# A transformer block on one core: transfers, the condition's path and weight slices of the first stage rearranged

## The chip, the cores and the metric

The kernel runs on one core of a Trainium2 chip. The metric is the device time of one execution in microseconds (us); lower is better. The engines of the core work side by side, each through its own queue in order: TensorE (PE; its weight loads are shown as PEld), VectorE (DVE), ScalarE (ACT), GpSimd (POOL) and SyncE (SP), which issues most DMAs. ScalarE and POOL issue DMAs too.

## The reference

A transformer block with a condition (adaptive layer norm), 2 batches of 2048 tokens, width D = 512, 16 heads of 32, hidden width 2048, all in f32:

```python
mod = silu(condition) @ Wada + bada
sh_a, sc_a, gt_a, sh_m, sc_m, gt_m = split(mod, 6, axis=1)
xm = layernorm(x, g1, be1) * (1.0 + sc_a[:, None, :]) + sh_a[:, None, :]
x = x + gt_a[:, None, :] * attention(xm, Wqkv, Wproj, bproj)     # causal
xm = layernorm(x, g2, be2) * (1.0 + sc_m[:, None, :]) + sh_m[:, None, :]
h = gelu(xm @ W1 + b1)
x = x + gt_m[:, None, :] * (h @ W2 + b2)
```

`condition` has 2 rows of 512, `Wada` is 512 x 3072, `Wqkv` 512 x 1536.

## The kernel before

The work is cut into tiles of 128 partitions (P). For each of the two batches there is a stage that computes queries, keys and values, then attention, then a projection; at the end comes the hidden layer for both batches. Products with weights are done by a scheme of seven products for eight (names A11, A12, A21, A22 for the four blocks of a weight, S1 to S4 for sums of blocks), so each weight block needs four sums, which POOL makes (`weight_sum`, L941) from the four loaded blocks. The change touches only the first stage, the queries, keys and values of batch 0 (L1359 to L1521).

Order: the program is written as a stream of operations; a framework places each on its engine's queue, inserts the waits, and may move an operation ahead of others on its engine, unless it is wrapped in `act` (L208), `mm` (L204) or `transpose` (L212), which keep the written order on that engine. Tiles of one tag share a fixed number of buffers, and a new one waits for the old one's last reader.

What the first stage does, in the order written:

- L89 to L152: constants, made by POOL and VectorE: the identity `ident`, masks, zeros. L136 is an activation with Sqrt on one column, `first`, that makes ScalarE load the table that holds Sqrt.
- L1363 to L1373: seven small DMAs from ScalarE's queue bring the condition (8 rows of 128), g1, be1, g2, be2, b1 and b2 as 44 rows of the tile `rows`.
- L1395 `load_x(0)`: four tiles of 128 x 512 of x, from SP. L1396 `load_wada(0, 1)`: two of the six column blocks of Wada as eight DMAs of 256 KB from SP into `vv`, and their bias from POOL into `mr`. L1397 `load_w` (L923): the four blocks of the query and key weights, 512 KB each, from SP into `wqk`. L1398 `load_wv` (L931): the value weights, four DMAs of 256 KB.
- L1400 to L1402: the 44 rows are transposed on TensorE into `ps_c` and copied to `cols`, where each vector stands as columns, by VectorE.
- L1450: for each of the four tiles of x the statistics (`stats` L216, VectorE); then `inv_std` (L223): Sqrt on ScalarE into `rstd`, its reciprocal and a product on VectorE. `scaled` (L958) normalizes the tiles on ScalarE in place, and `norm` (L970) transposes them into `ps_xt` on TensorE, in two halves of two tiles.
- L1454: Silu of the condition's columns into `sc` (ScalarE). `modulation(0)` (L1406): 16 matmuls of `sc` with Wada into `ps_mod`; `columns` (L1424): the bias added (`mr`, VectorE), eight small matmuls that turn rows into columns (`ps_modt`), a copy to `mod`. `scale_shift` (L1440) makes the factors a1 and c1 from `mod` and the columns of g1 and be1.
- L1464: `modulate` writes x, scaled, shifted and transposed, from `ps_xt` to `xmT`, even chunks on VectorE and odd ones on ScalarE. L1467: three sums of token halves (`t`, VectorE). L1469: the weight sums of columns 1 to 3 on POOL, four each; those of column 0 come later (L1477).
- L1520 `run` (L1138): for four groups of 512 tokens (g) and four weight columns of 128 (f) the products. The first column of the first group is done without the scheme (`plain`, L1086: 16 matmuls of 512 into `ps_qk`), the others with it (`unit`, L1002: seven products into banks named ps_a, ps_b, ps_c). Within `unit` the product S2 adds onto the bank of A11, after ScalarE has copied that bank out (L1059). Beside the products, `tick` (L1145) places the next group's loads of x, statistics, scaling and transposes, `also` (L1474) the later parts of the modulation, and `Pieces` (L1205) loads, sums and stores pieces of the hidden layer's weights.

Of the kernel before, what the change touches and what calls it, by code (L numbers as in the profile page):

```python
# [8 lines left out]
F32 = mybir.dt.float32  # L9
F32R = mybir.dt.float32r  # L10
BF16 = mybir.dt.bfloat16
AF = mybir.ActivationFunctionType
# [5 lines left out]
P = 128  # L18
# [9 lines left out]
def dit_block_kernel(  # L28
# [36 lines left out]
    nc = tc.nc  # L65
    B, T, D = x.shape
    HID = W1.shape[1]
    C = D // P
# [15 lines left out]
    def pool(name, bufs=1, **kw):  # L84
        return tc.tile_pool(name=name, bufs=bufs, reuse_waits="tile", **kw)
# [6 lines left out]
    ident = const.tile([P, P], F32, tag="ident", name="ident")  # L92
# [7 lines left out]
    eps = const.tile([P, 1], F32, tag="eps", name="eps")  # L100
# [16 lines left out]
    for n in range(2):  # L117

        f = bp.tile([P, QB + P], BF16, tag=f"fold{n}", name=f"fold{n}")
# [10 lines left out]
    def picks():  # L130
        two = ident.rearrange("p (k r b) -> p k r b", k=2, r=2)[:, :, :, :B]
        nc.vector.tensor_tensor(pickc, two[:, 0], two[:, 1], ALU.add)


    first = const.tile([P, 1], F32, tag="first", name="first")
    nc.scalar.activation(first, eps, AF.Sqrt)  # L136


    cols = const.tile([P, 64], F32, tag="cols", name="cols")
# [15 lines left out]
    n_cond = B * C  # L155
# [4 lines left out]
    n_rows = r_b2 + C  # L160
# [36 lines left out]
    def col(r, n):  # L197
        return cols[:, r : r + n]
# [9 lines left out]
    def act(ins):  # L208

        return tc.keep_in_program_order(ins)  # L210

    def transpose(dst, src):  # L212
        n = src.shape[0]
        return tc.keep_in_program_order(nc.tensor.transpose(dst, src, ident[:n, :n]))  # L214
# [78 lines left out]
    ps_sp = ps_s_cm.__enter__()  # L293
# [590 lines left out]
    w_v = Wqkv.rearrange("(c p) f -> p c f", p=P)  # L884
# [11 lines left out]
    HK = C // 2  # L896

    class Qkv:
# [21 lines left out]
                xts.append(xt)  # L920
            self.xts[g] = xts

        def load_w(self, queue):  # L923
            for n, i, k in BASE:
                act(
                    queue.dma_start(
                        self.w[:, n], w_v[:, k * HK : (k + 1) * HK, i * D : (i + 1) * D]
                    )
                )

# [429 lines left out]
    with pool("wada") as wp, pool("qkv0") as qp, pool("hl0") as hp, pool(  # L1360
        "ps_qkv0", bufs=6, space=PSUM
    ) as ps_mm:
        rows = wp.tile([n_rows, P], F32, tag="rows", name="rows")  # L1363
        for r, n, src in (
            (0, n_cond, cond.rearrange("b (c p) -> (b c) p", p=P)),
            (r_g1, C, g1.rearrange("(c p) -> c p", p=P)),
            (r_be1, C, be1.rearrange("(c p) -> c p", p=P)),
            (r_g2, C, g2.rearrange("(c p) -> c p", p=P)),
            (r_be2, C, be2.rearrange("(c p) -> c p", p=P)),
            (r_b1, FC, b1.rearrange("(c p) -> c p", p=P)),  # L1370
            (r_b2, C, b2.rearrange("(c p) -> c p", p=P)),
        ):
            nc.scalar.dma_start(rows[r : r + n, :], src)  # L1373
        wada_v = Wada.rearrange("(c p) f -> p c f", p=P)
        wada = {}

        def load_wada(s0, s1):
            w = row.vv[:, NT - 2 * C :].rearrange("p (n c) d -> p n c d", n=2)
            if s0 % 3 == 2:
                mr = modr  # L1380
            else:
                mr = wp.tile([P, D], F32, tag="mr", name="mr")
                nc.gpsimd.memset(mr, 0.0)
            for n, s in enumerate((s0, s1)):
                nc.gpsimd.dma_start(
                    mr[n * HD : n * HD + B, :],
                    bada[s * D : (s + 1) * D].partition_broadcast(B),
                )
            for k in range(C):
                for n, s in enumerate((s0, s1)):  # L1390
                    nc.sync.dma_start(w[:, n, k, :], wada_v[:, k, s * D : (s + 1) * D])
            wada[s0] = w, mr

        qkv = Qkv(row, qp, ps_mm)
        qkv.load_x(0)  # L1395
        load_wada(0, 1)  # L1396
        qkv.load_w(nc.sync)  # L1397
        qkv.load_wv(hp, nc.sync)  # L1398

        ps_c = ps_mm.tile([P, n_rows], F32, tag="mm", name="ps_c")  # L1400
        transpose(ps_c, rows)
        nc.vector.tensor_copy(cols[:, :n_rows], ps_c)  # L1402
        sc = wp.tile([P, C, HD], F32, tag="sc", name="sc")
        nc.vector.memset(sc, 0.0)

        def modulation(s0):  # L1406

            w, mr = wada.pop(s0)
            ps = ps_sp.tile([P, D], F32, tag="s", name="ps_mod")
            for k in range(C // 2):
                for half in range(2):
                    for n in range(2):
                        at = (2 * half + n) * HD
                        kk = half * C // 2 + k
                        mm(
                            ps[at : at + HD, :], sc[:, kk, :], w[:, n, kk, :],  # L1420
                            start=(k == 0), stop=(k == C // 2 - 1),
                        )

            def columns():  # L1424
                nc.vector.tensor_tensor(mr, ps, mr, ALU.add)
                if s0 % 3 == 2:
                    return
                ps_t = ps_sp.tile([P, C, 2, B], F32, tag="s", name="ps_modt")
                for k in range(C):
                    mm(  # L1430
                        ps_t[:, k], mr[:, k * P : (k + 1) * P], pickc,
                        start=True, stop=True,
                    )
                nc.vector.tensor_copy(
                    mod[:, s0 : s0 + 2], ps_t.rearrange("p c s b -> p s c b")
                )

            return columns

        def scale_shift(a, c, r_g, r_be, shift, scale):  # L1440

            for dst, r in ((a, r_g), (c, r_be)):
                nc.vector.scalar_tensor_tensor(
                    dst, mod[:, scale], 1.0,
                    col(r, C).unsqueeze(2).to_broadcast([P, C, B]),
                    ALU.add, ALU.mult,
                )
            nc.vector.tensor_tensor(c, c, mod[:, shift], ALU.add)

        for t in range(MTT):  # L1450
            qkv.stats(0, t)
        halves = [qkv.norm(0, 0, True)]

        act(  # L1454
            nc.scalar.activation(
                sc[:, :, :B], col(0, n_cond).rearrange("p (b c) -> p c b", c=C), AF.Silu
            )
        )
        picks()
        columns = modulation(0)  # L1460
        halves.append(qkv.norm(0, 1, True))
        columns()
        scale_shift(a1, c1, r_g1, r_be1, 0, 1)
        for k in range(0, C, 2):  # L1464
# [62 lines left out]
    with pool("qkv1") as qp, pool("ps_qkv1", bufs=6, space=PSUM) as ps_mm:  # L1527
        qkv = Qkv(row, qp, ps_mm)
# [62 lines left out]
    with ExitStack() as mlp:  # L1591
        wp = mlp.enter_context(pool("mlpw", side="right"))
        ps_mm = mlp.enter_context(pool("ps2", bufs=4, space=PSUM))
# [733 lines left out]
```

## Time and profile before

| what | value |
|---|---|
| median of 3 runs | 2258.96 us |
| the three runs | 2259.01, 2258.96, 2256.35 us |
| the profiled execution's own time | 2256.73 us |
| its span, first to last instruction | 2255.0 us |
| mean granted TensorE clock | 0.997 |
| instructions | 33464 |

The profile shows one execution. Times in it are us from the start of the span, unless marked ns. "busy" counts instructions at work, not issuing of DMAs or waiting. In a timeline a row gives start, length, engine, line of the kernel, operation, the tile written <- the tiles read, how many were merged, and in brackets the idle time of the engine before it and what ended it. An engine name with q (SPq, ACTq) is its sequencer, here issuing DMAs. In the stage table each engine has its busy time and its number of instructions; the last three columns are the granted TensorE clock, the busy share of the 16 DMA engines and GB/s. What ended a wait is inferred: where several were waited for, the one that came last by the profile is named.

### The profile page before, as it was taken

To read this page: it belongs to the slowest core of one execution; us is meant where nothing else is said; L and a number is where in the kernel's file an instruction comes from. 1 tells how busy PE (TensorE), PEld (TensorE's weight loads), DVE (VectorE), ACT (ScalarE), POOL (GpSimd) and SP (SyncE) were. 2 spreads that over 40 slices of the span, in tenths; PEclk is the share of its full clock that TensorE was granted. 3 is DMA by queue.
4 is the path that set the end of the run, shared out by engine and by line. 5 is a ranking of instruction groups with operands and counts; after the bars stand their busy time and mean duration, and the time that the engine had idled before them with its cause. 6 is when DMAs were issued, how large, how long until landed. Compare 5 with 4: busy or idle time off the path is not lost.

```text
span 2255.0 us, 33464 instructions
## 1 busy us (share of the span) xinstructions
PE 2211.3 (98%) x12057; PEld 1432.2 (64%) x12057; DVE 1535.7 (68%) x3309; ACT 1004.6 (45%) x2012; POOL 1297.9 (58%) x807
## 2 busy tenths in 40 slices
PE   7999999999999999999999999999999999999998
PEld 6777555555543587855555555345787787688687
DVE  4668766777757666777577767663685586576576
ACT  4434555555564244365656555614322422332410
POOL 4253998998983695199989898444205204304210
PEclk9999999999999999999999999999999999999999
DMA  8877143231324799542324113363353354353433
GB/s 281 251 259 193 43 93 75 62 85 48 106 97 135 252 308 313 142 92 62 85 67 104 44 48 131 109 231 129 109 175 133 123 184 145 108 187 126 158 125 110
DMA packets 160510, 311.57 MB, mean 138 GB/s; under 512 B 16544, under 2 KB 48844, under 8 KB 158552
## 3 DMA queue, kind: packets, MB, share of 16 engines
q1 hardware_dynamic: 155488, 285.53, 41.8%
q0 software_dynamic: 4480, 23.36, 2.7%
q8 instruction: 95, 1.56, 0.3%
q14 instruction: 71, 0.58, 0.1%
q10 hardware_dynamic: 376, 0.55, 0.1%
HBM read 229.95 MB, written 87.29 MB: 141 GB/s over the span
## 4 chain that ended last, share of the span: by engine, by line
PE 89%; DVE 4%; DMA 2%; POOL 2%; ACT 1%; issue 1%; SPq 0%; DVEq 0%; ACTq 0%; POOLq 0%
PE ps_a L206 27%; PE st L206 18%; PE ps_b L206 12%; PE o L206 10%; PE s L206 9%; PE ps_c L206 4%; PE ps_o L206 4%; PE sm L206 3%; DVE junk L498 1%; POOL ee L695 1%; PE ps_xt L214 1%; DMA x<-in_x_dram 1%; ACT e L670 1%; DVE mx L504 1%; PE ps_o L214 1%
## 5 line engine op out<-in xcount | busy, mean ns | idle before, releaser
L670 ACT ACTIVATE e<-st 128x512 f32<-128x512 f32 (+1 forms) x1152 | 575.0, 579 | 362.4 <-PE st L206 321.3
L504 DVE TENSOR_REDUCE mx<-s 128x1 f32<-128x512 f32 x576 | 381.9, 686 | 199.0 <-PE s L206 197.9
L695 POOL TENSOR_TENSOR ee<-ee,e 128x2048 f32<-128x2048 f32 x106 | 485.8, 4583 | 10.3 <-ACT e L670 4.3
L206 PE MATMUL st<-qst,kst 128*128 128x512 f32 (+3 forms) x1280 | 408.7, 386 | 0.0
L206 PE MATMUL s<-kst,qst 128*128 128x512 f32 (+3 forms) x1046 | 382.2, 396 | 8.0 <-DVE mx L498 2.7
L206 PE MATMUL ps_a<-sum,w 128*128 128x256 f32 (+1 forms) x1088 | 328.8, 431 | 0.1
L206 PE MATMUL o<-e,vv 128*32 128x512 f32 (+3 forms) x2560 | 293.2, 537 | 0.3 <-POOL e L682 0.3
L206 PEld LDWEIGHTS st<-qst,kst 128*128 128x128 f32 x1280 | 228.5, 188 | 97.3 <-issue 65.7
L498 DVE CUSTOM_DVE_ANT_0 junk<-s,causal 128x128 bf16<-128x128 f32 (+3 forms) x470 | 220.7, 470 | 61.0 <-PE s L206 46.8
L1795 POOL TENSOR_TENSOR sum<-w 128x256 f32<-128x256 f32 x30 | 21.8, 727 | 397.1 <-DMA w<-w1d 203.1
L206 PEld LDWEIGHTS s<-kst,qst 128*128 128x128 f32 x1046 | 195.4, 189 | 72.4 <-DVE mx L504 15.4
L206 PEld LDWEIGHTS ps_a<-sum,w 128*128 128x128 f32 x1088 | 204.5, 190 | 40.1 <-issue 11.4
L695 POOL TENSOR_TENSOR ee<-e 128x2048 f32<-128x2048 f32 x42 | 192.5, 4583 | 43.5 <-ACT e L670 42.5
L206 PEld LDWEIGHTS <-sel 32*128 32x128 bf16 x1152 | 29.5, 91 | 197.0 <-issue 196.1
L2014 ACT ACTIVATE h<-h,cols 128x512 f32<-128x512 f32 x120 | 76.8, 710 | 136.3 <-DVE h L1716 136.3
L504 DVE TENSOR_REDUCE mx<-st 128x1 f32<-128x512 f32 x192 | 131.0, 682 | 0.5
L682 POOL TENSOR_SCALAR_AFFINE_SELECT e<-e 128x512 f32<-128x512 f32 x128 | 83.3, 669 | 67.2 <-ACT e L670 67.2
L206 PE MATMUL st<-fold,sel 32*128 32x512 bf16 (+1 forms) x1152 | 117.3, 372 | 1.2
L206 PEld LDWEIGHTS o<-e,vv 128*32 128x32 f32 x2560 | 59.1, 108 | 92.3 <-issue 72.8
L1716 DVE TENSOR_TENSOR h<-c,ps_b 128x256 f32<-128x256 f32 x90 | 37.9, 421 | 103.5 <-PE ps_b L206 103.0
L1066 POOL TENSOR_TENSOR lo<-lo,hi 128x512 fp32r<-128x512 f32 x32 | 40.7, 1274 | 114.2 <-ACT hi L1064 109.8
L206 PE MATMUL ps_b<-sum,w 128*128 128x256 f32 (+1 forms) x384 | 95.0, 383 | 0.0
(237 smaller groups left out, 3590.7 us busy)
## 6 DMA issues: line engine op xcount, KB each, us to landing
qst<-q SPq DMA_DIRECT2D x128, 256.0 KB
kst<-k SPq DMA_DIRECT2D x128, 256.0 KB
w<-w1d SPq DMA_DIRECT2D x32, 896.0 KB
w<-w2d SPq DMA_DIRECT2D x28, 1024.0 KB
w<-w2d SPq DMA_DIRECT2D x28, 768.0 KB
q<-hi SPq DMA_DIRECT2D x32, 256.0 KB
q<-lo SPq DMA_DIRECT2D x32, 256.0 KB
k<-hi SPq DMA_DIRECT2D x32, 256.0 KB
```

Of the source, the lines that this page charges most:

```text
L206: return tc.keep_in_program_order(nc.tensor.matmul(*args, **kw))
L214: return tc.keep_in_program_order(nc.tensor.transpose(dst, src, ident[:n, :n]))
L498: nc.vector.tensor_tensor_reduce(junk[:, :w], x, causal[:, QB - w :], 1.0, MASKED, ALU.add, ALU.max, m,)
L504: self.vector(nc.vector.tensor_reduce(m, x, axis=AX.X, op=ALU.max))
L670: act(nc.scalar.activation(e4[:, h, :w], sts[h][:, :w], AF.Exp))
L682: nc.gpsimd.affine_select(d, d, pattern=[[0, HC], [1, P]], compare_op=ALU.is_ge, fill=0.0, base=0, channel_multiplier=-1,)
L695: act(nc.gpsimd.tensor_tensor(dst, x, y, ALU.add))
L1066: engine.tensor_tensor(lo, d, hi.bitcast(F32), ALU.subtract)
L1716: act(nc.vector.tensor_tensor(dst, x, y, ALU.add))
L1795: act(engine.tensor_tensor(dst, u, v, op))
L2014: nc.scalar.activation(d[j], d[j], AF.Gelu, bias=col(r_b1 + half * HF + fs[j], 1))
```

## The change

- The condition gets a tile of its own, `rows_c`, filled by the first DMA of ScalarE's queue; the eight small DMAs are kept in order. Behind them stands an activation with Silu on `first` in place of the one with Sqrt at the start.
- The query and key weights are loaded in three slices of columns: column 0, column 1, then columns 2 and 3, so twelve DMAs from SP instead of four (4 x 128 KB, 4 x 128 KB, 4 x 256 KB).
- TensorE transposes the identity into a scratch bank 6 times, then the 8 rows of the condition (`ps_1`), then the identity 32 times more (`busy`). Silu reads `ps_1` at once; behind it an activation with Sqrt on `first`. All of this is written ahead of the statistics.
- The transposes of all 44 rows (`ps_c`) and their copy to `cols` are written behind the modulation's matmuls and the second half of the transposes of x, just ahead of `columns`.

```diff
     first = const.tile([P, 1], F32, tag="first", name="first")
-    nc.scalar.activation(first, eps, AF.Sqrt)
...
-        def load_w(self, queue):
+        def load_w(self, queue, f=slice(0, D)):
             for n, i, k in BASE:
                 act(
                     queue.dma_start(
-                        self.w[:, n], w_v[:, k * HK : (k + 1) * HK, i * D : (i + 1) * D]
+                        self.w[:, n, :, f],
+                        w_v[:, k * HK : (k + 1) * HK, i * D + f.start : i * D + f.stop],
                     )
                 )
...
         rows = wp.tile([n_rows, P], F32, tag="rows", name="rows")
+        rows_c = wp.tile([n_cond, P], F32, tag="rowsc", name="rowsc")
...
-            nc.scalar.dma_start(rows[r : r + n, :], src)
+            if not r:
+                act(nc.scalar.dma_start(rows_c, src))
+            act(nc.scalar.dma_start(rows[r : r + n, :], src))
+        act(nc.scalar.activation(first, eps, AF.Silu))
...
-        qkv.load_w(nc.sync)
+        for f0, f1 in ((0, 1), (1, 2), (2, C)):
+            qkv.load_w(nc.sync, slice(f0 * P, f1 * P))
         qkv.load_wv(hp, nc.sync)
 
-        ps_c = ps_mm.tile([P, n_rows], F32, tag="mm", name="ps_c")
-        transpose(ps_c, rows)
-        nc.vector.tensor_copy(cols[:, :n_rows], ps_c)
+        ps_w = ps_sp.tile([P, P], F32, tag="s", name="ps_w")
+
+        def busy(n):
+            for _ in range(n):
+                transpose(ps_w, ident)
+
+        busy(6)
+        ps_1 = ps_sp.tile([P, n_cond], F32, tag="s", name="ps_1")
+        transpose(ps_1, rows_c)
...
+        act(
+            nc.scalar.activation(
+                sc[:, :, :B], ps_1.rearrange("p (b c) -> p c b", c=C), AF.Silu
+            )
+        )
+        act(nc.scalar.activation(first, eps, AF.Sqrt))
+        busy(32)
         for t in range(MTT):
             qkv.stats(0, t)
         halves = [qkv.norm(0, 0, True)]
 
-        act(
-            nc.scalar.activation(
-                sc[:, :, :B], col(0, n_cond).rearrange("p (b c) -> p c b", c=C), AF.Silu
-            )
-        )
         picks()
         columns = modulation(0)
         halves.append(qkv.norm(0, 1, True))
+        ps_c = ps_mm.tile([P, n_rows], F32, tag="mm", name="ps_c")
+        transpose(ps_c, rows)
+        nc.vector.tensor_copy(cols[:, :n_rows], ps_c)
         columns()
         scale_shift(a1, c1, r_g1, r_be1, 0, 1)
```

## The prediction

> **What bounds the kernel now.** I read the page first, then the stages, then the chain and the timeline of the first 30 us. In the page: busy time by engine, and the chain that ended last.
>
> ```profile
> PE 2211.3 (98%) x12057; PEld 1432.2 (64%) x12057; DVE 1535.7 (68%) x3309; ACT 1004.6 (45%) x2012; POOL 1297.9 (58%) x807
> ...
> PE 89%; DVE 4%; DMA 2%; POOL 2%; ACT 1%; issue 1%; SPq 0%; DVEq 0%; ACTq 0%; POOLq 0%
> ```
>
> TensorE is busy 98% of 2255.0 us, so the whole kernel is bound by TensorE, and the change removes none of its work. All it can bring is an earlier start of the unbroken work. The stage table (busy time per stage, PE first, granted clock third from the end) shows where that is.
>
> ```profile
> 18.12:27.86 9.74, 8.86 (x24) 4.50 (x25) 9.43 (x19) 4.66 (x10) 9.41 (x12) 1.00 0.90 296
> 27.86:74.90 47.04, 47.03 (x234) 39.97 (x235) 22.25 (x51) 21.63 (x49) 13.27 (x15) 1.00 0.73 238
> ...
> 119.50:126.20 6.70, 6.34 (x16) 5.08 (x17) 4.80 (x14) 0.82 (x2) 2.57 (x3) 0.52 0.58 202
> ```
>
> From 27.86 on PE has no gap for 47 us. Thus **27.86 us**, the start of the product S2 of the second weight column, is the number to move; 0.88 us of 18.12 to 27.86 is idle (9.74 less 8.86). Two things lead there. The first is the condition's path. In the timelines (start, length, engine, line, what; in brackets idle time and its releaser), ScalarE up to 13 us:
>
> ```profile
> 3.60 0.69 ACTq L1373 DMA_DIRECT2D rows<-in_L_cond_b_dram  x2
> 4.32 1.28 ACT L136 ACT_TABLE_LOAD   x1 [4.32 <-DMA x<-in_x_dram]
> ...
> 7.42 0.30 ACT L224 ACTIVATE rstd<-mv,eps 128x4 f32<-128x4 f32 x1 [1.61 <-DVE mv L221]
> 8.32 1.52 ACT L964 ACTIVATE x<-x,shift,rstd 128x512 f32<-128x512 f32 x2 [0.60 <-DVE shift L226]
> 9.86 1.28 ACT L1455 ACT_TABLE_LOAD   x1
> 11.15 0.21 ACT L1455 ACTIVATE sc<-cols 128x8 f32<-128x8 f32 x1
> 11.27 1.50 ACT L964 ACTIVATE x<-x,shift,rstd 128x512 f32<-128x512 f32 x2
> ```
>
> TensorE, with the one weight load that waits for a transfer, and VectorE's step between the matmuls:
>
> ```profile
> 9.89 1.76 PE L214 MATMUL ps_xt<-ident,x 128*128 128x128 f32 x7 [0.23 <-ACT x L964]
> 11.58 2.75 PE L206 MATMUL ps_mod<-vv,sc 128*32 128x512 f32 x16
> 14.26 1.09 PE L214 MATMUL ps_xt<-ident,x 128*128 128x128 f32 x8
> 15.29 1.05 PE L206 MATMUL ps_modt<-pickc,mr 128*128 128x4 f32 x8
> 18.12 7.13 PE L206 MATMUL ps_qk<-xmT,wqk 128*128 128x512 f32 x16 [1.78 <-DVE xmT L269]
> ```
>
> ```profile
> 12.89 0.12 PEld L206 LDWEIGHTS ps_mod<-vv,sc 128*32 128x32 f32 x1 [0.26 <-DMA vv<-in_L_cond_Wada_dram]
> ...
> 14.54 0.69 DVE L1425 TENSOR_TENSOR mr<-ps_mod,mr 128x512 f32<-128x512 f32 x1 [6.26 <-PE ps_mod L206]
> ```
>
> The Silu table load stands between the two pairs of scaled tiles, the modulation's matmuls wait for the last of Wada at 12.89, and from their end at 14.33 everything follows in a row: mr, ps_modt, a and c, xmT, ps_qk at 18.12. The second thing is ScalarE just ahead of 27.86, with the VectorE statistics that rstd waits for and POOL's weight sums:
>
> ```profile
> 25.91 1.28 ACT L224 ACT_TABLE_LOAD   x1
> 27.20 0.30 ACT L224 ACTIVATE rstd<-mv,eps 128x4 f32<-128x4 f32 x1
> 27.40 0.36 ACT L1059 ACTIVATE lo<-ps_a 128x256 f32<-128x256 f32 x1
> ```
>
> ```profile
> 25.35 1.25 DVE L218 BATCH_NORM_STATS2 stat<-x 128x6 f32<-128x512 f32 x2
> 26.52 0.29 DVE L221 BATCH_NORM_AGGREGATE mv<-stat 128x2 f32<-128x6 f32 x2
> ...
> 18.43 10.36 POOL L944 TENSOR_TENSOR wqk<-wqk 128x256 f32<-128x256 f32 x12 [0.18 <-DMA wqk<-in_L_cond_Wqkv_dram]
> ```
>
> S2 adds onto the bank that ScalarE copies out (lo<-ps_a) until 27.76. The chain of waits names POOL's weight sums as what ended the wait at 27.86, but the sums for this column are the first four of twelve begun at 18.43, done by 18.43 + 4 x 0.86 = 21.9; the copy's end fits within 0.1 us. I take the copy as the bound, and the Sqrt load and rstd ahead of it as its cause.
>
> **The change part by part.** *Small transfers and Silu first.* ScalarE issues one DMA more and then loads Silu's table and, behind sc, Sqrt's, both ahead of rstd of the first group. Issues end at 4.29 + 0.35 = 4.64; load, first, sc, load, first (each as long as sc): 1.28 + 0.21 + 0.21 + 1.28 + 0.21 = 3.19, so rstd at 7.8 instead of 7.42. With the 0.90 from rstd to the first scaled tile as now, the tiles run from 8.7 to 11.8 without the load between them, against 12.77 before. Three loads become two: Sqrt's table is still there at 25.91, so that load goes. The added wait is TensorE's for the condition's own rows, the first DMA issued; behind it stand the idle transposes on TensorE and sc, Sqrt's load and rstd on ScalarE. The bound is 0 to what lies beyond 5.9, when Silu's table is there; I take 0, since the x tile issued at the same 0.81 was read at 3.60 (the last row of this prediction).
>
> *TensorE kept busy.* 38 transposes, from the identity on:
>
> ```profile
> 1.41 0.29 POOL masks.py:199 TENSOR_SCALAR_AFFINE_SELECT ident<-ident 128x128 f32<-128x128 f32 x1
> ```
>
> Seven cold ones took 1.76 us (0.25 each), so at most 9.5 us from 1.7 on, done by 11.2; at the later rate (eight in 1.09) by 7. Behind them wait the first group's transposes, ready at 9.5, and the matmuls of the modulation, which Wada holds to 12.89 anyway. Cover 1.7 us, cost nothing. With them the matmuls run at the later rate:
>
> ```profile
> 67.20 1.92 PE L206 MATMUL ps_mod<-vv,sc 128*32 128x512 f32 x16
> ```
>
> From 12.89 to 14.33 are 1.44 us; times 1.92/2.75 that is 1.0, so ps_mod ends at 13.9, **0.43 earlier**. The bound is 0 (Wada later by that much: one more small DMA lies before it) to 1.4 (no wait on Wada at all); I keep Wada where it is, since its 2 MB stand behind the same x loads.
>
> [...]
>
> *Rows transposed behind the modulation.* ps_c joins TensorE's queue between eight transposes (about 1.0) and ps_modt, at 0.1 to 0.30: they end at 13.9 + 1.0 + 0.1 = 15.0; mr is done at 13.9 + 0.2 + 0.69 = 14.8. So ps_modt starts at 15.0 instead of 15.29 and **0.3 of the 0.43 is left**. The copy to cols (0.20) lies beside ps_modt's 1.05 on VectorE; queued ahead of mr it would cost up to 1.2. ps_qk starts at 17.8; S2 could start at 27.86 - 0.88 - 0.3 = 26.7.
>
> *Weights by columns.* Twelve DMAs instead of four, packets of 512 B and 1 KB instead of 2 KB. SP issues them, and wv and the next x tiles queue behind.
>
> ```profile
> 0.81 2.38 SPq L919 DMA_DIRECT2D x<-in_x_dram  x4
> 4.22 3.79 SPq L1391 DMA_DIRECT2D vv<-in_L_cond_Wada_dram  x8
> 8.05 2.47 SPq L926 DMA_DIRECT2D wqk<-in_L_cond_Wqkv_dram  x4
> 10.86 2.69 SPq L936 DMA_DIRECT2D wv<-in_L_cond_Wqkv_dram  x4
> 14.29 4.39 SPq L919 DMA_DIRECT2D x<-in_x_dram  x4
> ```
>
> Issue: 12 x 0.62 = 7.4 from 8.05, to 15.5; wv to 18.2, x to about 20 at the first x's rate. Its issue so ends 1.3 later than now (18.7). Transfer: three answers of the DMA view, for 13 to 16 us (2 KB packets), 18.7 to 20.5 (1 KB) and 54.6 to 55.6 (512 B), give packets, MB and share of 16 engines, and the last row the queues' load from 24 to 26 us in 40 slices:
>
> ```profile
> q1 hardware_dynamic: 607, 1.17, 103.5%
> ...
> q1 hardware_dynamic: 631, 0.63, 109.6%
> ...
> q1 hardware_dynamic: 379, 0.18, 75.7%
> ...
> DMA  7110000000000000064979999799796890032722
> ```
>
> Share times 16 times length by MB is 42, 50 and 67 us of engine per MB. 1.05 MB at 67 and 1.05 MB at 50 instead of 42 cost (25 + 8) x 1.05 / 16 = 2.2 us; if the 512 B row holds idle time, all at 50, 1.1. The queues run empty at 24.15 now, so x of the second group is in by then, and would be by 25.2 to 26.4. The last of its statistics starts at about 25.95. So VectorE, which could be 0.3 earlier, is about held where it is: mv at 26.8, nothing gained or lost, and 0.4 later at the worst of it. The earlier first columns serve POOL's sums, which are not late, and ps_qk, which waits for xmT. The second half's sums start about 1 later than now by the same price; POOL's next work, the value sums, is behind them in either case.
>
> *S2.* rstd at 26.86 without the load, lo from 27.06 to 27.42, S2 at 27.5: **0.35 earlier**. If rstd is queued behind lo, 26.7: 1.2 earlier. I take 0.7, between these. Sum: 2256.73 - 0.7 = 2256.0 for the profiled execution; that one lies 2.2 below the median of the three runs, 2258.96, which gives **2258.3**. From 27.86 to 74.9 PE has no gap in which this could be lost, and later stages are paced by PE.
>
> **The rivals.** *Nothing arrives:* mv comes 0.4 later with x and takes the load's place, or rstd still needs its own load because ScalarE takes it ahead of sc. For it: VectorE is busy 9.43 of 9.74 us. 2259.0.
>
> *More than forecast:* Wada in at 12.4, S2 at 26.0, 1.9 gained, and besides the half-clock stretch 119.5 to 126.2 vanishes (granted clock 0.52; 6.34 us of PE work that at 1.00 would take 3.3): 1.9 + 3.1 = 5.0, so 2254.0. It speaks against it that nothing there is touched. [...]
>
> *Slower: SP's issue becomes the bound.* At another place the same kind of piece (128 x 2 rows of 512 B) took far longer to issue:
>
> ```profile
> 52.04 1.99 SPq L1230 DMA_DIRECT2D vv<-in_L_cond_W_dram  x4
> ...
> 56.56 3.36 POOL L1251 TENSOR_TENSOR vv<-vv 128x256 f32<-128x256 f32 x4 [19.10 <-DMA vv<-in_L_cond_W_dram]
> ...
> 107.57 4.91 SPq L1230 DMA_DIRECT2D kst<-in_L_cond_W_dram  x4
> ...
> 3.60 0.69 DVE L218 BATCH_NORM_STATS2 stat<-x 128x6 f32<-128x512 f32 x1 [2.23 <-DMA x<-in_x_dram]
> ```
>
> At 1.23 each the twelve end at 22.8, wv at 25.5, x at 27.3; with 2.8 to land (the first x: issued at 0.81, read at 3.60, last row), statistics 0.85, rstd and lo 0.7, S2 comes at 31.6, 3.7 late, and a PE idle that long meets a half clock like the row of 0.52, 3.1 more: 2265.8. It decides from x landing after 26.0. Against it: 0.50 each at 52.04, and 0.62 each at 8.05 for twice the bytes.
>
> [...]
>
> **How the numbers follow.** Forecast 0.50, nothing 0.25, more 0.14, slower 0.11. Three runs lie 2.7 us apart; about 0.2%, 4.5 us, is what can be told from no change, so the first two cases are "same": 0.75, faster 0.14, slower 0.11. The range must leave out 2 in 10 at most and reach toward both outer cases: 2253.8 to 2262.0; forecast and nothing alone 2256 to 2260.
>
> **What would show it.** Right: only two table loads before 30 us; ps_mod ends at about 13.9 and ps_qk starts at about 17.8; S2 at 26.7 to 27.5, with lo<-ps_a ending just ahead; x of the second group landing 1 to 2 later. Wrong: a third load, cols' copy ahead of mr, S2 later than 27.9 behind a late x, a different stretch of half clock.

## The result and the profile after

The changed kernel takes **2262.23 us** (median of 12 runs, 2260.07 to 2266.9) beside 2257.57 for the kernel before (12 runs, 2254.0 to 2260.75): ratio 1.0024, interval [1.0017, 1.0032] (ratios here are of means, and so differ a little from those of the medians). It is slower by 4.7 us; forecast were 2258.3, a range of 2253.8 to 2262.0, and no change that can be told. The profiled execution took 2261.88 us, with a span of 2260.2 and a mean granted clock of 0.996.

On the page, TensorE's share and the chain that ended last read almost as before:

```profile
PE 2221.8 (98%) x12096; PEld 1439.1 (64%) x12096; DVE 1536.4 (68%) x3309; ACT 1003.5 (44%) x2012; POOL 1296.1 (57%) x807
...
PE 89%; DVE 5%; POOL 2%; DMA 2%; ACT 2%; issue 1%; SPq 0%; ACTq 0%; DVEq 0%; POOLq 0%
```

TensorE's timeline in the changed kernel shows where the time went:

```profile
10.74 4.02 PE L205 MATMUL ps_mod<-vv,sc 128*32 128x512 f32 x16
...
15.90 1.05 PE L205 MATMUL ps_modt<-pickc,mr 128*128 128x4 f32 x8
19.76 9.82 PE L205 MATMUL ps_qk<-xmT,wqk 128*128 128x512 f32 x16 [2.81 <-DVE xmT L268]
...
33.94 1.10 PE L205 MATMUL ps_a<-t,wqk 128*128 128x256 f32 x4 [2.63 <-POOL wv L949]
35.48 2.04 PE L205 MATMUL ps_b<-xmT,wqk 128*128 128x256 f32 x4 [0.45 <-ACT lo L1059]
```

S2 of the second weight column starts 6.08 us late, at 33.94 in place of 27.86: 1.64 because ps_qk starts later (19.76 for 18.12), 2.69 because it takes 9.82 for 7.13, and the rest in front of S2. The third of these rows is the first clue: the same 16 matmuls take longer. The stages (busy time and count for PE, PEld, DVE, ACT, POOL; granted clock third from the end) say why:

```profile
14.99:18.40 3.41, 1.97 (x17) 1.66 (x15) 2.10 (x6) 0.00 (x0) 1.15 (x2) 1.00 1.01 308
18.40:21.81 3.41, 2.05 (x3) 1.02 (x4) 3.27 (x7) 1.93 (x4) 3.03 (x6) 0.50 1.01 329
32.05:35.47 3.42, 1.10 (x4) 0.69 (x5) 2.05 (x7) 1.78 (x5) 3.42 (x4) 1.00 0.95 262
35.47:38.88 3.41, 3.40 (x8) 2.78 (x9) 0.43 (x1) 2.25 (x4) 0.77 (x2) 0.50 0.65 178
119.50:126.20 6.70, 6.32 (x36) 3.69 (x35) 5.58 (x13) 1.77 (x4) 2.80 (x4) 1.00 0.98 315
```

Twice a stretch in which TensorE has little to do is followed by one at half clock: on ps_qk, and again behind the wait for S2. The last row is the other side: the half clock of the kernel before at 119.5 to 126.2 (0.52, 16 matmuls) is not there, 36 matmuls run instead, and with the stall ahead of it about 4.6 us come back. It is not shown that the change does this: in three further profiles in which nothing or little is changed of the kernel before (e8, e13 and e16 below), this halved stretch lasts 3.41 us in the first two and is missing in the third. TensorE, 8.4 us behind at 40 us and 3.8 at 130, is 3.6 behind at its end; the last store comes another 1.5 later behind it than in the profile of before.

What S2 waits for stands in ScalarE's timeline. Two table loads are left, as forecast; but see what follows rstd:

```profile
4.63 1.28 ACT L1377 ACT_TABLE_LOAD   x1 [4.63 <-DMA rows<-in_L_cond_g_dram]
...
6.21 1.28 ACT L223 ACT_TABLE_LOAD   x1
...
33.27 0.30 ACT L223 ACTIVATE rstd<-mv,eps 128x4 f32<-128x4 f32 x1 [3.05 <-DVE mv L220]
33.47 0.36 ACT L1059 ACTIVATE lo<-ps_a 128x256 f32<-128x256 f32 x1
34.26 0.82 ACT L964 ACTIVATE x<-x,shift,rstd 128x512 f32<-128x512 f32 x1 [0.42 <-ACT lo L1059]
34.98 0.36 ACT L1059 ACTIVATE lo<-ps_b 128x256 f32<-128x256 f32 x1
```

rstd waits for VectorE (mv) until 33.27, and the copy of ps_a stands behind it, until 33.83: that is what S2 waits 2.63 us for (its row names a sum of wv, which S2 does not read). Besides, **a scaled tile of x now stands ahead of the copy of ps_b**, for which S4 waits until 35.48. In the kernel before both copies came ahead of the tiles; the lines that follow its copy of ps_a at 27.40:

```profile
27.67 0.37 ACT L1059 ACTIVATE lo<-ps_b 128x256 f32<-128x256 f32 x1
28.08 1.52 ACT L964 ACTIVATE x<-x,shift,rstd 128x512 f32<-128x512 f32 x2
```

VectorE and POOL in the changed kernel, where mv was held up:

```profile
17.29 0.71 DVE L1454 SCALAR_TENSOR_TENSOR c<-mod,cols 128x8 f32<-128x8 f32 x1
18.03 0.65 DVE L1459 TENSOR_TENSOR c<-c,mod 128x8 f32<-128x8 f32 x1
...
21.32 6.03 DVE L997 TENSOR_TENSOR t<-xmT,t 128x512 f32<-128x512 f32 x2
...
30.74 1.61 DVE L997 TENSOR_TENSOR xmT<-xmT 128x512 f32<-128x512 f32 x1
...
33.05 0.18 DVE L220 BATCH_NORM_AGGREGATE mv<-stat 128x2 f32<-128x6 f32 x1
```

```profile
17.25 2.89 POOL L944 TENSOR_TENSOR wqk<-wqk 128x256 f32<-128x256 f32 x4 [11.85 <-DMA wqk<-in_L_cond_Wqkv_dram]
...
21.44 2.08 POOL L944 TENSOR_TENSOR wqk<-wqk 128x256 f32<-128x256 f32 x3
23.48 0.54 POOL L1389 DMA_DIRECT2D mr<-in_L_cond_bada_dram  x1
24.03 3.90 POOL L944 TENSOR_TENSOR wqk<-wqk 128x256 f32<-128x256 f32 x5
```

Read the two together: operations of 8 elements take 0.7 us, and two sums of token halves 6.03 (2.16 before), while POOL runs sum behind sum at 0.72 each. The first of the two ends when POOL stops for its DMA.

mv ends at 33.23 in place of 26.81, 6.4 us late. On VectorE xmT starts 1.64 later (1.04 of it are the two operations c), the first three token sums take 3.7 more, the fourth (30.74) 0.9 more: together 6.3. No row of VectorE up to there waits for x.

### The profile page after: what moved, and what is told of

Same layout as the page of the kernel before. It is cut to its first block, busy times and chain, and to the rows that moved or that the text cites. A ratio compares the mean times of both kernels' runs of the same rounds, so it can differ in the third digit from the quotient of the medians.

```text
span 2260.2 us, 33554 instructions
## 1 busy us (share of the span) xinstructions
PE 2221.8 (98%) x12096; PEld 1439.1 (64%) x12096; DVE 1536.4 (68%) x3309; ACT 1003.5 (44%) x2012; POOL 1296.1 (57%) x807
## 3 DMA queue, kind: packets, MB, share of 16 engines
q1 hardware_dynamic: 157664, 285.53, 41.8%
## 4 chain that ended last, share of the span: by engine, by line
PE 89%; DVE 5%; POOL 2%; DMA 2%; ACT 2%; issue 1%; SPq 0%; ACTq 0%; DVEq 0%; POOLq 0%
PE ps_a L205 27%; PE st L205 19%; PE ps_b L205 12%; PE o L205 10%; PE s L205 9%; PE ps_c L205 4%; PE sm L205 3%; PE ps_o L205 2%; PE ps_xt L213 1%; POOL ee L694 1%; DVE junk L497 1%; ACT e L669 1%; DVE mx L503 1%; DVE stat L217 1%; PE ps_o L213 1%
```

## The experiments

All ratios are against the kernel before, run in turn on the same chip; its median was 2257.4 to 2257.9 in each group. The runs up to e9 were on one chip, e10 to e13 on a second, e14 to e17 on a third. e7 and e8 leave out a part of the result.

| run | what it is | median us | ratio, interval |
|---|---|---|---|
| e1 | changed, no idle transposes | 2266.23 | 1.0041 [1.0028, 1.0053] |
| e2 | changed, whole weight transfers | 2265.89 | 1.0037 [1.0024, 1.0049] |
| e3 | changed, neither of the two: condition's part alone | 2264.20 | 1.0028 [1.0016, 1.0040] |
| e4 | before + columns | 2259.43 | 1.0012 [1.0003, 1.0021] |
| e5 | before + idle transposes | 2261.04 | 1.0020 [1.0011, 1.0029] |
| e7 | changed, no weight sums | 2259.46 | 1.0008 [0.9999, 1.0017] |
| e8 | before, no weight sums | 2257.00 | 0.9997 [0.9988, 1.0006] |
| e9 | changed, x first, sums held | 2260.16 | 1.0013 [1.0004, 1.0022] |
| e10 | changed + filled wait | 2260.98 | 1.0014 [1.0006, 1.0023] |
| e11 | e3, value sums held | 2266.91 | 1.0036 [1.0023, 1.0048] |
| e12 | e9 + statistics in place + filled wait | 2258.67 | 1.0000 [0.9991, 1.0009] |
| e13 | before, a second profile | 2259.81 | one run |
| e14 | changed + statistics in place | 2260.37 | 1.0015 [1.0006, 1.0024] |
| e15 | e3 + statistics in place | 2262.14 | 1.0019 [1.0010, 1.0028] |
| e16 | before + statistics in place | 2259.09 | 1.0008 [0.9999, 1.0017] |
| e17 | changed + statistics in place + filled wait | 2256.53 | 0.9999 [0.9990, 1.0008] |

**One part taken out, one part alone.** Three theories: the clock is halved where the work begins (A), POOL's sums hold up VectorE (B), or the transfers of Wada or of x come late (C).

e1 and e2, then e5 (to the kernel before); e4 is the kernel before with the change's three slices:

```diff
-        busy(6)
-        busy(32)
```

```diff
-        for f0, f1 in ((0, 1), (1, 2), (2, C)):
-            qkv.load_w(nc.sync, slice(f0 * P, f1 * P))
+        qkv.load_w(nc.sync)
```

```diff
+        ps_w = ps_sp.tile([P, P], F32, tag="s", name="ps_w")
+        for _ in range(38):
+            transpose(ps_w, ident)
         ps_c = ps_mm.tile([P, n_rows], F32, tag="mm", name="ps_c")
         transpose(ps_c, rows)
```

> The changed kernel without its 38 idle transposes (6 and 32 of the identity). Theory A, the clock: the early transposes raise the clock at 8 us, the thin stretch from 9 to 18 us is then taken as idle, and the halved clock falls on ps_qk (9.82 us there instead of 7.13). Then here ps_qk takes about 7.1 us, no halved clock stands between 14 and 30 us, and the time is 2.5 to 5 us below the changed kernel's, 2257 to 2260. Theory B, POOL's sums: by columns they start while VectorE makes c and the token sums and hold it up; then c still takes 0.7 and the token sums 2 to 3 us each, S2 starts at 30 us or later and the time stays over 2260. Theory C, the transfers: Wada in at 13.7 instead of 12.9 and x of the second group at 27 instead of 24; then ps_mod ends at 14.7 as in the changed kernel.

> The changed kernel with the query and key weights loaded whole again (four DMAs of 512 KB). Theory A: the halved clock is still there, ps_qk takes 9 us or more, S2 is at 30 us or later, the time 2260 to 2262. Theory B: POOL's sums start behind 18 us, c and its sum take 0.2 each, the token sums about 1 us each; xmT starts at 17.1 to 17.6, and S2 follows ps_qk without the wait of 2.6 us: the time is 2 to 4 us below the changed kernel's. Theory C: x of the second group is in at about 24 instead of 27, and S2 is not held by its statistics.

> The kernel before with nothing but the weights by columns. Theory A: no halved clock before 30 us, the time within 1 us of before. Theory B: POOL's sums start at 16.5 to 17.5, VectorE's small operations ahead of xmT or its token sums (1.0 us each before) take 2 us or more, S2 starts 1.5 to 4 later than 27.9, the time is 1.5 to 4 us above before. Theory C: the same sign, by x of the second group in at 26 to 27, with token sums of about 1 us.

> The kernel before with nothing but 38 idle transposes ahead of the transposes of the rows. Theory A: the clock is raised by 9 us and halved again somewhere between 15 and 26, ps_qk takes 8.5 to 10 us instead of 7.1, the time is 2.5 to 5 us above before. Theories B and C: nothing is added to VectorE, POOL or the queues: ps_qk at or ahead of 18.1 us, the time within 1 us of before or 0.5 below.

None of the three predicted that with either part taken out the kernel is slower still. e4 came out as B forecast: 1.8 us above the kernel before, POOL's sums from 17.94, one c at 0.58, S2 at 30.85. But its ps_qk took 8.83 us, in part at half clock, without any idle transposes, which A as written did not allow. e5 came out as A forecast in time (3.4 above) and ps_qk (9.93), but it is confounded (there the condition's rows stand behind the idle transposes, and mr comes at 16.64), so it says little about idle transposes as such. And e1 shows B at work in another place. VectorE's fourth token sum and POOL's value sums there:

```profile
28.37 4.72 DVE L997 TENSOR_TENSOR xmT<-xmT 128x512 f32<-128x512 f32 x1
33.02 0.17 DVE L220 BATCH_NORM_AGGREGATE mv<-stat 128x2 f32<-128x6 f32 x1
```

```profile
28.84 5.38 POOL L949 TENSOR_TENSOR wv<-wv 128x512 f32<-128x512 f32 x4
```

A sum of 0.72 us (24.62 before) takes 4.72, mv and rstd stand behind it, and S2 comes at 34.68.

**The condition's part alone, and the sums left out.** e7 and e8 leave out POOL's weight sums of batch 0 (products that need a sum read block A11); e9 tries a remedy. e3 has the edits of e1 and e2 together; e7 and e8, where the sums' functions return at once for batch 0, and e9, with x of the second group issued ahead of weight columns 2 and 3, a small copy on POOL ahead of column 1's sums and one ahead of the rest. P in the expectations is B for single operations: VectorE's operations on two tiles in SBUF stand still while POOL's sums run back to back.

```diff
-                        ps, self.w[:, n, k, f * P : (f + 1) * P], ops[n][:, k],
+                        ps, self.w[:, self.used(n), k, f * P : (f + 1) * P], ops[n][:, k],
...
+        def used(self, n):
+            return A11 if self.row.b == 0 and n in (S1, S2, S3) else n
```

```diff
...
         halves.append(qkv.norm(0, 1, True))
+        qkv.load_x(1)
+        qkv.load_w(nc.sync, slice(2 * P, D))
+        qkv.load_wv(hp, nc.sync)
...
+        act(nc.gpsimd.tensor_copy(hold, c1[:, 0, :1]))
...
+                act(nc.gpsimd.tensor_copy(hold, qkv.xmT[0][:, 0, HALF_T : HALF_T + 1]))
```

> The changed kernel without the 38 idle transposes and with the four whole weight transfers: the condition's own tile, its early transpose and Silu, and the late transposes of all rows are left. Forecast of the prediction for this part alone: a gain of 0.4 to 0.7, 2256.9 to 2257.6. P: x is issued as in the run with whole transfers (15.5, landing at 23 and later), VectorE's statistics of the second group come later than before, so its fourth token sum meets POOL's sums and takes over 2 us; rstd at 30 to 34, S2 behind it; 2260 to 2266. A: without idle transposes the clock rises at about 13 as before, so nothing is halved before 30 us; 2257 to 2258.

> The changed kernel without POOL's sums of the query, key and value weights in the first stage (products that need a sum read the block A11 instead, so this part of the result is left out; every matmul stays). After the first four runs the theories stand thus. P (VectorE's sums of two tiles in SBUF stand still while POOL's weight sums run back to back): the two operations c take 0.16 us each as before, the four token sums about 0.7 each, xmT starts at about 17.7 in place of 18.71; the statistics of the second group then wait only for x (last landing 26.95), rstd comes at 29.0 to 29.5 in place of 33.27, S2 of the second weight column at 29.3 to 29.8 in place of 33.94; time 2257.0 to 2259.5. A (the clock's halving alone makes the loss): S2 still behind 32 or the halved 18.4 to 25.2 left with its full cost; 2260.5 to 2262.5. C (x of the second group lands too late): S2 not under 31; 2260 to 2262.

> The kernel before, with the same sums left out (the same part of the result). P: the first three token sums, 0.81, 1.03 and 1.10 us before, take 0.7 each, rstd of the second group still stands behind Sqrt's table load, so S2 at 27.2 to 27.9 and 2256.0 to 2257.8; the changed kernel without sums is then less than 2 us above this one, where the two differ by 4.7 with the sums. A and C: as before, 2257 to 2258, and the distance to the changed kernel without sums stays 4 us or more.

> The changed kernel with the transfers of x for the second group issued behind weight columns 0 and 1 (columns 2 and 3 and the value weights behind them), POOL's sums of column 1 held behind the second operation c, and all later sums held behind the fourth token sum of VectorE. P and C together: c 0.16 each, token sums about 0.7 but for one that may meet the sums of column 1, x landed by about 21, rstd by 26, S2 at 26.5 to 28.5; 2254 to 2258. P alone without C would give the same here but a much later S2 in the kernel without sums (that is, S2 there at 29 or later only by x). A: the halved clock stays on ps_qk, which takes 9.8 us for 7.1, 2258 to 2261.

e7 and e8 came out by P in time (2259.46 and 2257.00), but 2.5 us apart, where P had less than 2. So 2.2 of the 4.7 us are gone without the sums (2.8 by e7's own median). VectorE in e7, then in e8:

```profile
17.79 0.17 DVE L1466 TENSOR_TENSOR c<-c,mod 128x8 f32<-128x8 f32 x1
...
20.59 1.42 DVE L1004 TENSOR_TENSOR t<-xmT,t 128x512 f32<-128x512 f32 x2
...
25.14 0.69 DVE L217 BATCH_NORM_STATS2 stat<-x 128x6 f32<-128x512 f32 x1 [2.78 <-DMA x<-in_x_dram]
...
29.46 0.18 DVE L220 BATCH_NORM_AGGREGATE mv<-stat 128x2 f32<-128x6 f32 x1
```

```profile
23.12 0.69 DVE L218 BATCH_NORM_STATS2 stat<-x 128x6 f32<-128x512 f32 x1 [0.31 <-DMA x<-in_x_dram]
```

The same operations take 0.17 and 0.71 each with POOL at rest. And x of the second group arrives 2.0 us later in the changed kernel (25.14 against 23.12), and with the sums gone VectorE waits 2.78 us for it, though C's "S2 not under 31" did not come. mv in e7 is at 29.46 in place of 33.05, and S2 at 30.30, a little past the 29.8 expected:

```profile
30.30 1.13 PE L205 MATMUL ps_a<-t,wqk 128*128 128x256 f32 x4 [0.71 <-ACT lo L1066]
```

In e9 the statistics slid ahead of the condition's operations on VectorE, which then stood until x came at 19.50; xmT came at 21.42, and the time was missed.

e3 shows the strongest case, and makes a new question. VectorE, POOL and ScalarE:

```profile
30.27 3.92 DVE L225 SCALAR_TENSOR_TENSOR shift<-mv,rstd 128x4 f32<-128x4 f32 x1
```

```profile
30.46 3.70 POOL L949 TENSOR_TENSOR wv<-wv 128x512 f32<-128x512 f32 x3
34.11 0.54 POOL L1389 DMA_DIRECT2D mr<-in_L_cond_bada_dram  x1
```

```profile
29.81 0.36 ACT L1059 ACTIVATE lo<-ps_a 128x256 f32<-128x256 f32 x1
34.26 0.81 ACT L964 ACTIVATE x<-x,shift,rstd 128x512 f32<-128x512 f32 x1 [4.09 <-issue]
34.98 0.36 ACT L1059 ACTIVATE lo<-ps_b 128x256 f32<-128x256 f32 x1
```

Four columns of 128 numbers take 3.92 us, to the moment when POOL turns to its DMA. The scaled tile waits for them ("issue": its releaser was not found, but its start follows shift's end at 34.19), the copy of ps_b waits behind the tile, and TensorE's S4 behind the copy (35.49). This part alone, forecast by the prediction's terms as a gain of 0.4 to 0.7, costs 6.4 us.

**The clock, the value sums, and a second look at before.**

e10 (to the changed kernel) and e11 (to e3; the value sums are written behind it). e12 is e9 with the edits of e10 and e14; e13 is the kernel before.

```diff
         columns()
+        busy(24)
         scale_shift(a1, c1, r_g1, r_be1, 0, 1)
```

```diff
+                act(nc.gpsimd.tensor_copy(hold, shift1[:, MTT : MTT + 1]))
+                qkv.value_weight_sums()
```

> The changed kernel with 24 more idle transposes on TensorE behind ps_modt, where it waits for xmT. In the runs so far the granted clock is set anew every 3.41 us, and every window of 3.41 us in which TensorE was busy less than about 2 us was followed by a halved one. W (that rule): the window that ended at 18.4 with 1.97 us of work gets over 1 us more, the clock is not halved on ps_qk, which takes 7.1 to 7.3 us in place of 9.82 and ends near 27; but S2 of the second column stays at 32 to 34, since VectorE's chain (P) holds it and not ps_qk, and TensorE only waits longer: 2260 to 2262.5. If the halved clock on ps_qk were what costs the time (A): 2258 to 2259.5.

> The run with the condition's part alone, with the four POOL sums of the value weights held behind the shift of the second group on VectorE (a POOL copy of one column of it stands ahead of them). There the operation shift, 128x4 elements, began at 30.27 and took 3.92 us while three value sums ran from 30.46 to 34.11. P: shift takes 0.16 to 0.3 us, the scaled tiles of x start at about 31 in place of 34.26, ScalarE's copy of ps_b behind them at about 31.5 in place of 34.98; the halved windows from 30.6 to 40.8 become fewer; 2258 to 2261.5 in place of 2264.2. If something other than POOL's sums holds that operation: it stays above 2 us and the time at 2263 to 2265.

> The run with x ahead of weight columns 2 and 3 and held sums, mended twice: there the statistics of the second group slid ahead of the condition's operations on VectorE and stood waiting for x until 19.5, so that xmT came at 21.42. Here they keep their written place behind the second weight column's first products, and 24 idle transposes fill TensorE's wait for xmT. P, C and W together: c 0.17 each, xmT at 17.9 to 18.2, ps_qk at 19.0 to 19.3 for 7.1 us, S2 of the second column no longer behind rstd, at 26.5 to 28.0, no halved clock from 15 to 40 us: 2253 to 2257. If W is wrong: ps_qk takes 9 to 10 us and 2257 to 2260.

> The kernel before once more, unchanged, for a second execution with a profile. W: the windows of the clock begin at another moment against the program, so the halvings lie elsewhere than at 119.1 and 876.9; where one that begins between 13 and 20 us ends inside the wait for xmT, ps_qk is halved as in the other runs. The token sums of VectorE take 0.7 to 1.2 us as in the first profile, since POOL's sums then wait for their weights. Span 2252 to 2260.

W, the rule of the clock that e10's expectation states, held there. Stages of e10, then TensorE in e10:

```profile
15.00:18.40 3.40, 3.40 (x31) 3.18 (x30) 2.09 (x6) 0.00 (x0) 1.25 (x2) 1.00 0.95 292
18.40:21.81 3.41, 3.40 (x17) 2.09 (x16) 3.27 (x7) 1.93 (x4) 2.59 (x5) 1.00 0.98 317
28.40:31.80 3.40, 0.14 (x1) 0.00 (x0) 2.83 (x5) 0.38 (x2) 3.40 (x4) 1.00 0.76 230
31.80:35.21 3.41, 1.13 (x3) 0.98 (x4) 0.69 (x1) 3.41 (x7) 3.33 (x4) 0.50 0.72 240
```

```profile
19.68 7.13 PE L205 MATMUL ps_qk<-xmT,wqk 128*128 128x512 f32 x16
...
34.08 2.04 PE L205 MATMUL ps_a<-t,wqk 128*128 128x256 f32 x4 [5.54 <-issue]
```

With the wait filled, ps_qk runs in 7.13, and S2 stays at 34.08: TensorE just waits 5.54 us there, and meets the half clock behind that wait. The 2.7 us won on ps_qk are lost again in the same place; 1.2 are left in the median, which the intervals do not tell from nothing.

The kernel before has no right to its whole clock either. e13, the same program, stages and ps_qk:

```profile
14.71:18.12 3.41, 2.37 (x20) 1.82 (x16) 1.59 (x6) 0.00 (x0) 0.68 (x2) 1.00 1.05 385
18.12:21.53 3.41, 2.67 (x3) 1.18 (x4) 3.41 (x5) 1.93 (x4) 3.32 (x6) 0.50 1.09 357
```

```profile
18.86 10.13 PE L206 MATMUL ps_qk<-xmT,wqk 128*128 128x512 f32 x16 [1.78 <-DVE xmT L269]
```

Here ps_qk takes 10.13, S2 is at 31.61, and the run 2259.81. Its xmT comes 0.74 later than in the profile that the prediction was made from (17.81 against 17.07). Over the four profiles with that part as before (before, e8, e13, e16), xmT begins between 17.07 and 18.44, so the prediction's base was the best of them.

e11 missed: holding the value sums moved the four sums of column 0 into their place (POOL at 29.83, 2.76 us), shift took 2.30 in place of 3.92, ending with them, and the copies stayed behind the tile. That agrees with P on which operations are held up and shows that holding one group of sums is no remedy. It also left the order of ScalarE's queue as the thing to try.

**The queues' order.** e14 to e17: one line keeps the second group's statistics at their written place on VectorE; both of ScalarE's copies then come ahead of rstd and the tiles, where the kernel before had rstd first. D in the expectations: the loss is the new order of ScalarE's queue.

```diff
-                            self.stats(g + 1, n - 10)
+                            self.stats(g + 1, n - 10, row.b == 0 and g == 0)
```

> The changed kernel with one edit: the statistics of the second group keep their written place on VectorE (behind the first products of the second weight column). In the changed kernel ScalarE's queue reads rstd, copy of ps_a, one scaled tile of x, copy of ps_b; before it reads rstd, copy of ps_a, copy of ps_b, scaled tiles. With the edit the copies come first. D (the loss is the new order of the queues: TensorE's S2 and S4 stand behind rstd and behind a scaled tile, and so behind VectorE's chain): S2 of the second column goes to 28 to 31.5, right behind ps_qk and A11 and S1, S4 follows without a gap, no halved clock from 35 to 39; 2257 to 2260 in place of 2262.2. P alone (POOL's sums delay VectorE wherever they meet): c and token sums are as slow as in the changed kernel, and the time stays at 2261 to 2263.

> The same edit on the run with the condition's part alone, which took 2264.2 with S2 at 30.27, S4 at 35.49 behind the scaled tile, and a halved clock from 30.7 to 40.9. D: S2 at 27 to 28.5, S4 right behind, no halved clock there; 2256.5 to 2259.5. If the loss came from POOL's sums alone or from the late x: 2262 to 2265.

> The same edit on the kernel before, as the fair base of the two runs above. D: its ScalarE queue had the copies ahead of the scaled tiles already, so only the wait of 0.88 us for rstd goes: S2 at 26.9 to 27.3 in place of 27.86 where ps_qk starts at 18.1; 2256.0 to 2258.5, not told from the kernel before.

> The changed kernel with the statistics in place and 24 idle transposes in TensorE's wait for xmT. D and W together: ps_qk at 19.6 to 19.9 for 7.1 us, S2 at 28.3 to 28.8, no halved clock from 15 to 40 us: 2255.5 to 2258.5. Beside the run with x first and held sums (2258.67), whose S2 came at 27.67, it shows what holding POOL's sums is worth when the queues' order is mended: under 1 us by D, 2 to 4 us by P.

TensorE in e14, and in e17, from ps_qk to S2 and S4 of the second column:

```profile
19.94 10.02 PE L205 MATMUL ps_qk<-xmT,wqk 128*128 128x512 f32 x16 [2.80 <-DVE xmT L268]
...
31.52 1.03 PE L205 MATMUL ps_a<-t,wqk 128*128 128x256 f32 x4
32.39 1.03 PE L205 MATMUL ps_b<-xmT,wqk 128*128 128x256 f32 x4
```

```profile
19.25 7.03 PE L205 MATMUL ps_qk<-xmT,wqk 128*128 128x512 f32 x16
...
27.85 1.03 PE L205 MATMUL ps_a<-t,wqk 128*128 128x256 f32 x4
28.71 1.03 PE L205 MATMUL ps_b<-xmT,wqk 128*128 128x256 f32 x4
```

In e14 TensorE has no wait from ps_qk on, although c takes 0.70 and 0.65 us and two token sums 6.03 as in the changed kernel: those delays now hurt only ps_qk's start. That is D's mechanism; S2 (31.52) and the time (2260.37) lie just past what D expected. The edit moves the median by 1.9 us there and by 2.1 in e15 (2262.14 against 2264.20; 2256.5 to 2259.5 was expected, but ps_qk was halved, 9.99 us, and a second half clock followed at 41.8). Each time the intervals overlap, so it is the traces that show the step, and not the times. On the kernel before the edit gains nothing (e16: 2259.09, where 2256.0 to 2258.5 was expected).

With the clock window filled as well, e17 reaches 2256.53, 0.9 below its base where the changed kernel is 4.7 above its own. It is not to be told from the kernel before, and it is faster than the changed kernel clear of noise ([0.9990, 1.0008] against [1.0017, 1.0032]). So the order and the filled wait together remove the loss. e12, with x moved and the sums held besides, is not better (2258.67; S2 at 27.67 and ps_qk at 7.03 came as expected, the 2253 to 2257 did not): with these two mended, holding POOL's sums won nothing that can be told, as D had it. No version beat the kernel before. What is won at 40 us need not last, either: TensorE in e17 leads the profile of before by 2.9 us at 130 us and is level with it at the end; a halved stretch near 876 us lasts 3.41 in that profile of before, 6.83 in e17 and 10.24 in e10.

## Why the prediction was wrong, step by step

- **What bounds.** That S2 stands behind rstd and the copy of ps_a was right; with that wait gone, in e16, S2 follows S1 without a gap. But S2's start was taken for the number to move as if only this wait and xmT entered it; it moved the wrong way by both and by the clock.
- **Silu first, table loads.** Right: two loads, rstd at 7.51 (7.8 forecast), scaled tiles from 8.25 to 11.18 (8.7 to 11.8).
- **"cost nothing"** for the idle transposes: right as a direct cost (done at 9.4, cover until Wada). That they bring the matmuls to the later rate was the author's estimate, from rows of two different moments; the changed kernel shows it for transposes of 128x128: 421 ns up to 8.0 us and 273 from there on, where the kernel before has 421 up to 11.2 and 273 from 14.3. But ps_mod ended at 14.76, not 13.9: with TensorE ready earlier, its weight loads waited four times for pieces of Wada, the last at 13.71 against 12.89. "I keep Wada where it is" missed by 0.8 us in this pair of profiles, and the 0.43 is not seen. But Wada comes at another moment in each execution: ps_modt starts at 15.29, 16.05, 16.04 and 16.69 in the four profiles with this part as before (before, e13, e16, e8). So it is not shown that the change made it later, nor that it gained the 0.3.
- **Rows behind the modulation.** Order right (cols behind mr); ps_modt at 15.90 for 15.0, by Wada's arrival.
- **Weights by columns.** Issue at 0.63 each and x 1 to 2.2 later: right (2.0). Here is the step that failed: VectorE "is about held where it is: mv at 26.8, nothing gained or lost, and 0.4 later at the worst", since the early columns "serve POOL's sums, which are not late". mv came at 33.05. Early, the columns let POOL start at 17.25 with four sums in a row, onto the two operations c (1.0 us more, all of it on the path to ps_qk) and the token sums (6.03 for 2.16). Without the sums mv is at 29.46 and S2 at 30.30 (e7), and there VectorE does wait for the late x. Not what POOL waits for, but what POOL then holds up, had to be priced: the working has VectorE wait for x alone.
- **S2, "I take 0.7".** The chain behind this term held: mv, rstd at 33.27, the copy of ps_a at 33.47, S2 at 33.94. But with mv fixed the choice was between two places of rstd, both of them a gain. It also took the rest of the queue's order as fixed while an instruction of 1.28 us was taken out of it. The order is made anew: ahead of the copy of ps_b now stands a tile that waits for VectorE's shift, and S4 waits behind it. e14 and e15 point to about 2 us for S2 and S4 waiting on VectorE, e7 to 2.2 to 2.8 for the sums; each alone is at the edge of the noise, and the two overlap and do not add up.
- **The clock.** It was a rival's side effect; it should have been a term: ps_qk's 9.82 for 7.13 is 2.69 of the 6.08 by which S2 is late. Every halved stretch here lasts one or several times 3.41 us (but for one at the very end that the last instruction cuts off), starting at other moments in each execution: 6.83 from 119.11 and 3.41 from 876.87 in the profile of before, 6.83 from 18.38, 3.41 from 35.44 and 6.83 from 878.54 in the changed kernel. On that grid of 3.41 us, from the clock's first rise on, over the whole of before and of the changed kernel, the first 45 us of e1, e2, e4 and e5 and the stages of e10, all 13 windows in which TensorE was busy for 1.41 us or less were followed by a halved one (1.41 us in before, then 0.50; 1.16 in e1, then 0.51; 0.14 in e10, then 0.50); from 1.63 to 2.67 both occur (1.63 in e2 and 2.67 in e13, then 0.50; 2.01 in before and 2.67 in the changed kernel, then 1.00), so the "about 2 us" of e10's expectation was no sure bound. In the changed kernel the wait for xmT sits in a window with 1.97 us of work; filled, in e10, e12 and e17, it is followed by a whole clock each time. By the medians that is worth 1.2 us where S2 waits anyway (e10 against the changed kernel, within the noise) and 3.8 where it does not (e17 against e14).
- **The slower rival** had the consequence (S2 late, then a half clock; 31.6 and 2265.8) by a cause that did not occur: the twelve transfers were issued at 0.63, not 1.23. **"More than forecast"** was half right in its oddest term: the half clock at 119.5 did vanish, and 4.6 us came back, in a kernel that had lost 8.4; as e8, e13 and e16 have it shorter or not at all, that may be luck.
- The base of 2256.73 minus a gain was also a lucky execution: early xmT and a whole clock on ps_qk, which e13 did not have.

Not settled: why all three parts together (2262.2) lose less than the condition's part with either one (2265.9 to 2266.2) or alone (2264.2). In each, VectorE meets POOL at another instruction and the clock windows fall elsewhere; two profiles of one kernel differ by as much, and the intervals of e3 and the changed kernel overlap. Open too is how the loss divides between POOL's sums, the late x, the order and the clock.

## What to carry to other kernels

Where a scheduler orders the queues, an instruction taken out can reorder what follows: before pricing a gain, ask what would stand ahead of the operation that TensorE waits for, and pin that order. Price work on POOL by VectorE's operations beside it, and an early start as carefully as a late one. Count TensorE's work in each 3.41 us around a wait; a wait that leaves it half empty can cost a halved clock behind it as well (1.10 us of work here, then 3.41 us at 0.50), and one profile of the base is too few to see that.

## What the runs showed of the hardware

VectorE's operations with two inputs in SBUF were held up beside POOL's sums: 128x512 sums of 0.7 us took up to 4.72 (e1), shift (128x4) 3.92 (e3; 0.16 in e7, with POOL at rest), c (128x8) 0.71 (changed kernel; 0.16 in e7). Not each time: in e3 the token sum at 28.02 took 0.67 while four of POOL's sums ran from 25.72 to 29.27. A 128x512 copy with one input (pick) took 0.94 in the changed kernel for 0.42 in e7. Operations with one input in PSUM (xmT from ps_xt, 0.47 apart; lo from ps_qk, 0.67) and the statistics (0.66) kept their time, the same in both. The wait can outlast one of POOL's sums: in e3 shift was started at 30.27, beside a sum of column 0, and stood through that and three value sums, until POOL paused at 34.11; the three took 3.70 us, 1.23 each, where four took 5.42 in the kernel before. The two c in the changed kernel took only 0.71 and 0.65, about one sum of 0.72 each, while the next sum followed at once. What decides how many sums VectorE waits for is not settled here.

The idle transposes do raise the clock earlier (at 8.1 us in the changed kernel, against 13.3 in the kernel before), but in the changed kernel it falls again behind the wait for xmT (at 18.4), where it stays whole in e10, e12 and e17 with that wait filled. Warming up 10 us ahead of the work earned nothing that these runs show.
